# Three more seven-product steps inside one layer of a two-layer LoRA kernel, and a new order for its side work

## The chip, the cores and the metric

The kernel runs on one core of a Trainium2 chip. The metric is device time in microseconds, from start to end of one execution. Three executions of the kernel before took 425.69, 426.36 and 426.70 us; the median is 426.36.

## What is computed

Two layers, each added to its input, in float32, on 8 sequences of 256 tokens with 1024 features.

```python
base   = x @ W.T                                   # W: 1024 x 1024
logits = x @ Wr.T + 5.0 * one_hot(language_ids[b]) # 8 experts
gates  = softmax over the two largest logits, zero elsewhere
h      = A[e] @ x                                  # e = 1..8, rank 16
x      = x + base + 2.0 * sum_e gates[e] * (B[e] @ h[e])
x      = x + x @ weight[adapter_ids[b]].T          # one 1024 x 1024 matrix per sequence
```

## The kernel before, in words

**Blocks.** Tokens, inner dimension and outputs are each cut in two, so the large product of layer one is a 2 x 2 by 2 x 2 block product. The blocks of x are `xb["11"]` to `xb["22"]`, those of W `wb[...]`, the results `yb[...]`. An identity is added to the diagonal blocks of W, so that adding x comes for free.

**Three levels of steps.** The block product is done with seven block products instead of eight (a Strassen-Winograd step); they are named 1, 2, 5, 6, 3, 7, 4 in the order in which they run. Product 1 is `opening` (L563), the others are `product` (L655). Each is itself such a step, with seven smaller products of 256 x 256 x 1024 blocks. Inside `product` these are P1 to P7 with sums s1 to s4 and t1 to t4, made on VectorE (DVE), and they accumulate in three PSUM pairs called A, X and B, which change their places from product to product (`roles`, L110). A small product is two k chunks by two row chunks, that is four matmuls of 512 columns. B3 and A4 are names of the small products that finish quarter 1 (in B) and quarter 2 (in A); A6 and A7 are P6 and P7, B5 is P5, X2 is P2.

**Third steps.** A few of the small products are cut once more: `third` (L412) replaces four 512-column matmuls by seven `piece`s of 256 columns (L449). It needs eight sums of its own on DVE: r1, r2, r4 (128 columns each) and q1, q2, q4 (256 columns) first, and r3, q3 once piece 5 has been read; and `take` (L467) evicts pieces 1, 6, 7 and 5 separately. "Leaf 2" is a third step on the small product with a(0,1) and b(1,0), "leaf 3" the one that is B3 (the small product P3), "leaf 4" the one that is A4. Pieces 1, 6 and 7 share a PSUM bank (`single0`, or one half of X), so piece 6 waits until piece 1 has been evicted, and piece 7 until piece 6 has. Before, twelve small products are cut so: leaves 3 and 4 in product 1, leaf 2 in products 2, 6 and 7, leaves 2, 3 and 4 in product 5, leaves 2 and 4 in products 3 and 4 (L994 to L1038).

**The order of the work.** Every engine runs its queue in order, and the order is fixed when the program is built. PE's order is the order of the calls in `product`. DVE's is made by a small planner (L346 to L393): `now["pe"]` and `now["dve"]` are estimated clocks, `queue` holds sums with a cost and the events that they need, `ahead(until)` fills DVE's time up to PE's clock with whatever is free, `force(key)` pulls a sum in when PE needs it, and `after` puts an eviction behind PE's clock. Costs and events only decide the order; at run time semaphores keep engines apart.

**Gates.** `project` (L248) computes h and the logits on PE for tokens (j, c), `take(j, c)` (L265) adds the language bias on DVE and copies h on ScalarE (ACT), `gating(j)` (L290) is 20 small operations that end with the scaling of h, and `turn(j)` (L323) transposes h with eight matmuls on PE and copies it to `hg`, where the LoRA matmuls (L551, `hg,b_sb` and `hg,bdiff`) read it. The first gates are turned before product 2, the second after it, in two single banks, `ps_g`.

**Other sums.** I22 adds an identity to w22, S1 forms w21 - w22, S2, S3 and S4 form other blocks of W, `bdiff` holds differences of the LoRA matrix. Before, I22, S1 and bdiff are queued with product 2's work (L1012 to L1014).

**Layer two** (`adapt`, L851) does one sequence after the other with one such step each. Its weights are loaded by SyncE (SP) into blocks of x and w that layer one has finished with (`load_w1`, L804), its sums for the first sequence are `prep_w1` and `prep_y0`. GpSimd (POOL) issues the DMAs that add: `add_x`, `add_raw` and `join`.

The calls in the order of time, with what is queued ahead of each:

```python
queue += [(0.69, (), "I22", lambda: add_identity(wb["22"]))]
queue += w_sum(minus, "21", "22", "21", (), "S1")
queue += [(2.0, (), "bdiff", b_differences)]
queue += make_subs("5", "21", "12", (2, 3, 4), ("T1",), "2", 1)
product("2", y21, y11, 0, 0)
force(gates)
turn(1, singles("ps_g_1"))
```

Of the kernel before, what the change touches and what calls it, by code (L numbers as in the profile page):

```python
# [25 lines left out]
def kernel(  # L26
# [43 lines left out]
    TQ = TH // 2  # L70
# [32 lines left out]
    def singles(name):  # L103
        return [single(f"{name}{v}", v) for v in range(2)]
# [185 lines left out]
    def gating(j):  # L290

        m1, hot1, ops1 = first_max(lg[j], j, 1)
        rest = rtile([P, C, E], "rest")
        m2, hot2, ops2 = first_max(rest, j, 2)
        dm = rtile([P, C], "dm")
        ex = rtile([P, C], "ex")
        den = rtile([P, C], "den")
        g1 = rtile([P, C], "g1")
        g2 = rtile([P, C], "g2")
        wide = [P, C, E]  # L300

        def onto_h():
            h = hT[j].rearrange("p c (e r) -> p (c e) r", r=R)
            g = hot1.rearrange("p c e -> p (c e)").unsqueeze(2).to_broadcast([P, C * E, R])
            tt(h, h, g, ALU.mult)


        ops = ops1 + [
            lambda: nc.vector.scalar_tensor_tensor(rest, hot1, NEG, lg[j], ALU.mult, ALU.add)
        ] + ops2 + [  # L310
            lambda: minus(dm, m2, m1),
            lambda: nc.scalar.activation(ex, dm, AF.Exp),
            lambda: nc.vector.tensor_scalar(den, ex, 1.0, None, ALU.add),
            lambda: nc.vector.reciprocal(g1, den),
            lambda: nc.vector.tensor_scalar(g1, g1, SCALING, None, ALU.mult),
            lambda: tt(g2, g1, ex, ALU.mult),
            lambda: tt(hot1, hot1, g1.unsqueeze(2).to_broadcast(wide), ALU.mult),
            lambda: tt(hot2, hot2, g2.unsqueeze(2).to_broadcast(wide), ALU.mult),
            lambda: add(hot1, hot1, hot2),
        ]  # L320
        return [(0.23, f) for f in ops] + [(1.22, onto_h)]

    def turn(j, banks):  # L323

# [21 lines left out]
    events = {}  # L346
    queue = []
    done = {}

    def us(n):  # L350
        return (n + 151) / 960

    def vec(t, fn, key=None):
        fn()
        now["dve"] += t
        done[key] = now["dve"]

    def event(name, later=0.0):
        events[name] = now["pe"] + later
# [5 lines left out]
    def ahead(until):  # L365

        while now["dve"] < until:
            may = [(t, i) for i, t in enumerate(map(free, queue)) if t is not None and t < until]
# [43 lines left out]
    def third(key, leaf, lhs, rhs, place, what):  # L412
# [10 lines left out]
        def op(name, tag, fn, x, y, what):  # L423
            width = P if name[0] == "r" else NQ

            def run():
                if place == 0:
                    t[name] = sub3.tile([P, width], F32, name=f"{name}_{key}{leaf}", tag=tag)
                else:
                    t[name] = spare(1536 + (place - 1) * 1152 + at[tag], width)  # L430
                fn(t[name], *(t[v] if isinstance(v, str) else v() for v in (x, y)))

            return us(width), what, f"{me}.{name}", run
# [42 lines left out]

        return ops, ops3, piece, take

    def make_subs(key, w, x, leaves=(), what=(), last=(), place=0):

# [5 lines left out]
        def a(i, j):  # L486
            return wb[w][:, 2 * j : 2 * j + 2, i * OQ : (i + 1) * OQ]
# [27 lines left out]
        if 3 in leaves:  # L515
            deep[3] = third(key, 3, lambda: t["s2"], lambda: b(1, 1), 1, (f"{key}:P6",))
        if 4 in leaves:
            deep[4] = third(key, 4, lambda: a(1, 1), lambda: t["t2"], 2, (f"{key}:P6",))
        subs[key] = (a, b, t, late, deep)
        return [  # L520
            op("s1", add, a(1, 0), a(1, 1), what),
# [17 lines left out]
    def multiply(up=None, tokens=None):  # L539


        def mm(acc, lhs, rhs, first=False, rows=None, c=0, part=(0, 1), ms=(0, 1), need=()):
            if rows == "d":
                force("bdiff")
            for key in need:
                force(key)
            steps = [(lhs[:, k, ts(m, P)], rhs[:, k, :], m) for k in part for m in ms] if part else []
            if up is not None and rows is not None:
                steps += [(up[rows][:, ts(m, P)], hg[tokens][:, c, :], m) for m in ms]
            for i, (l, r, m) in enumerate(steps):  # L550
                nc.tensor.matmul(  # L551
                    acc[:, m, :],
                    lhsT=l,
                    rhs=r,
                    start=(first and i < len(ms)),
                    stop=(i >= len(steps) - len(ms)),
                    skip_group_check=True,
                )
                now["pe"] += 0.859

        return mm

    def opening(key, dest):  # L563
# [56 lines left out]
        chunk(1)  # L620
        piece(6)
        out(6, q1, q1)
        chunk(2)
        for n in (2, 3, 4):
            piece(n, B)
# [1 line left out]
        piece(7)  # L627
        out(7, q1, q1)
        last_out = out
        ops, ops3, piece, out = third(key, 4, lambda: a(1, 1), lambda: t["t2"], 0, ())  # L630
        for o in ops[:2]:
            vec(o[0], o[3], o[2])
        last_out(5, q1, q1)
        for o in ops[2:]:
            vec(o[0], o[3], o[2])
        add(q1, B, q1)
        chunk(4)
        piece(1)
        out(1, q2)
        chunk(5)  # L640
        piece(5)
        for o in ops3:
            vec(o[0], o[3], o[2])
# [5 lines left out]
        chunk(7)  # L649
        piece(7)  # L650
        out(7, q2)
        out(5, q2, q2)
        add(q2, A, q2)

    def product(key, base, dest, lora=None, tokens=None, sub=False, joined=None):  # L655

# [61 lines left out]
        if 4 in deep:  # L718
            _, _, piece4, take4 = deep[4]
            piece4(1)  # L720
            take4(1, at[2], old[2], sub)
        if 3 in deep:
            _, _, piece, take = deep[3]
            force(f"{key}.X2")
            piece(1, banks=halves(X))
            take(1, at[1], at[1], sub)
            force(f"{key}.B5")
            mm(B, None, None, False, "d", 1, part=())
            piece(5, banks=halves(X))
            if 4 in deep:  # L730
                piece4(5)
            piece(6)
            take(6, at[1], at[1], sub)
            if 4 in deep:
                piece4(6)
                take4(6, at[2], old[2], sub)
            for n in (2, 3, 4):
                piece(n, B)
            if 4 in deep:
                force(f"{key}.A7")  # L740
                mm(A, None, None, False, "1", 0, part=())
            piece(7)
            take(7, at[1], at[1], sub)
            take(5, at[1], at[1], sub)
        else:
            mm(B, t["s2"], b(1, 1), False, "d", 1, need=K("s4", "B5"))
        put(1, B, True, "B3")
        join(1)
        if 4 in deep:
            if 3 not in deep:  # L750
                piece4(5)
                piece4(6)
                take4(6, at[2], old[2], sub)
# [8 lines left out]
        else:  # L762
            mm(A, a(1, 1), t["t2"], False, "1", 0, need=K("t4", "A7"))
            put(2, A, name="A4")
        join(2)
        ahead(now["pe"])


# [216 lines left out]

    opening("1", y21)
    done.clear()
    now["pe"], now["dve"] = 0.0, 3.5
    after(0.4, lambda: take(0, 1))
    for i, (t, f) in enumerate(gating(0)):  # L990
        vec(t, f, "gates0")
    project(1, 0, halves(pair("ps_h_1_0", 2)))
    now["pe"] += 7.5
    subs2 = make_subs("2", "12", "21", (2,))  # L994
    run(subs2[:2])
    after(0.4, lambda: take(1, 0))
    run(subs2[2:])
# [11 lines left out]
    event("T2", 30.0)  # L1009
    queue += [(t, (), f"gate{i}", f) for i, (t, f) in enumerate(gating(1))]  # L1010
    gates = queue[-1][2]
    queue += [(0.69, (), "I22", lambda: add_identity(wb["22"]))]  # L1012
    queue += w_sum(minus, "21", "22", "21", (), "S1")
    queue += [(2.0, (), "bdiff", b_differences)]  # L1014
    queue += make_subs("5", "21", "12", (2, 3, 4), ("T1",), "2", 1)
    product("2", y21, y11, 0, 0)
    force(gates)
    turn(1, singles("ps_g_1"))
    now["pe"] += 2.0
    raw("21", 0, 1)  # L1020
    add_raw("21", 1, 1)
    event("T3", 30.0)
    queue += w_sum(add, "11", "21", "11", (), "S2")
    queue += make_subs("6", "11", "22", (2,), ("T2",), "5", 0)
    product("5", None, y22, 1, 1)
    raw("12", 1, 1)
    event("x22", 14.0)
    queue += w_sum(minus, "12", "11", "12", (), "S4")
    queue += make_subs("3", "12", "12", (2, 4), ("x22",), "6", 1)
    product("6", y21, y21, sub=True)  # L1030
    add_raw("22", 1, 0)
# [3 lines left out]
    product("3", y22, y12, 2, 1, joined=(y12, y21))  # L1035
    load_w1(0, "21", "12", "22", "11")
    event("w0", 18.0)
    queue += make_subs("4", "22", "22", (2, 4), ("T4",), "7", 1)  # L1038
    product("7", y21, y21, joined=(y22, y21))
    queue += [(t, ("w0",), f"w0_{i}", f) for i, (t, _, f) in enumerate(prep_w1(0, 0))]  # L1040
    y0 = []

    def prep_y0(i):
        y0[:] = y0 or prep_y(0)
        y0[i][2]()

    queue += [(0.69, ("4:P7", "7:join2"), f"y0_{i}", lambda i=i: prep_y0(i)) for i in range(4)]
    product("4", y21, y21, 1, 0)
    for q in list(queue):
        q[3]()  # L1050
    load_w1(1, "22", "12", "11", "21")

    for u in range(NB):
        if u + 1 < NB:
            todo += prep_y(u + 1)
            todo += prep_w1(u + 1, 4)
        adapt(u)
# [50 lines left out]
```

## Time and profile before

| | before |
|---|---|
| three executions | 425.69, 426.36, 426.70 us |
| the profiled execution | 425.69 us, of which 423.7 us are the span of the instructions |
| PE matmuls | 418.8 us busy, 1294 records |
| PE weight loads | 226.1 us busy |
| DVE | 287.6 us busy, 439 instructions |
| ACT | 40.6 us busy |
| start of product 2, 5, 6 | 59.25, 90.62, 120.28 us |
| start of product 3, 7, 4 | 143.97, 174.05, 197.67 us |
| start of layer two | 227.75 us |
| end of the last matmul | 420.3 us |

A float32 matmul shows as two records. In the timeline of PE a row is "start, length, engine, line, operation, output<-inputs, sizes, number of records"; the length of a row reaches a little past the start of the next because matmuls are pipelined, so durations are taken from start to start. In a table of windows each engine has "busy (x instructions)", in the order PE, weight loads, DVE, ACT, POOL, and the last three columns are PE's granted clock, the busy share of the DMA engines and GB/s. DVE's most frequent forms, start to start where the next follows at once: 1.13 us for 1024 columns, 0.60 for 512 (0.72 where the next reads what it wrote), 0.34 for 256, 0.20 for 128.

### The profile page before, as it was taken

What the parts mean: (1) busy time and instruction counts of PE and PEld (TensorE: products, weight loads), DVE (VectorE), ACT (ScalarE), POOL (GpSimd) and SP (SyncE); (2) the same over time, 40 slices, a digit from 0 to 9 for tenths busy, and PEclk for the clock granted to TensorE, in tenths of its full rate; (3) what the DMA queues carried; (4) which work ended last, traced back from release to release, by engine and by line L of the source; (5) the groups of instructions that cost most, each with busy time, mean ns of one, the idle gap of its engine ahead of it and who ended that gap; (6) DMA issues with size and microseconds to landing.
All of it is one profiled execution on the core that took longest, in us unless ns stands there. A gap on an engine that the chain in (4) does not pass through costs nothing.

```text
span 423.7 us, 3569 instructions
## 1 busy us (share of the span) xinstructions
PE 418.8 (99%) x1294; PEld 226.1 (53%) x1294; DVE 287.6 (68%) x439; ACT 40.6 (10%) x69; POOL 17.6 (4%) x26
## 2 busy tenths in 40 slices
PE   8999999999999999999999999999999999999996
PEld 6579975445655454554555444444444444444574
DVE  1645699957888989878786666765747666665531
ACT  2010120022110000000000101010101101010110
POOL 1000020110001101103000000000000000000000
PEclk9999999999999999999999999999999999999999
DMA  8995089476220964918902384666658385650202
GB/s 274 385 397 236 2 173 210 126 184 101 100 99 4 179 215 78 294 24 155 342 0 99 116 321 159 242 214 213 224 194 300 109 298 190 213 183 0 101 0 99
DMA packets 20257, 72.61 MB, mean 171 GB/s; under 512 B 1552, under 2 KB 3856, under 8 KB 15248
## 3 DMA queue, kind: packets, MB, share of 16 engines
q1 hardware_dynamic: 15088, 58.87, 38.0%
q0 software_dynamic: 3904, 12.58, 16.6%
q10 hardware_dynamic: 1248, 0.93, 0.7%
q8 instruction: 10, 0.16, 0.1%
q14 instruction: 7, 0.06, 0.0%
HBM read 55.61 MB, written 8.39 MB: 151 GB/s over the span
## 4 chain that ended last, share of the span: by engine, by line
PE 99%; POOL 0%; ACT 0%; issue 0%; POOLq 0%
PE A L863 23%; PE A L551 21%; PE B L551 13%; PE B L863 13%; PE ps_h L256 7%; PE X L863 6%; PE P L463 5%; PE A_last L930 3%; PE X L551 3%; PE X L463 2%; PE A L463 1%; PE idle L568 1%; PE B L463 1%; PE ps_g L326 0%; ACT z L960 0%
## 5 line engine op out<-in xcount | busy, mean ns | idle before, releaser
L551 PE MATMUL A<-t,s 128*128 128x512 f32 x112 | 50.3, 592 | 0.0
L863 PE MATMUL B<-x,x 128*128 128x512 f32 x96 | 43.2, 592 | 0.0
L863 PE MATMUL A<-w,x 128*128 128x512 f32 x88 | 39.6, 592 | 0.0
L228 DVE TENSOR_TENSOR w<-w,w 128x1024 f32<-128x1024 f32 x24 | 29.1, 1223 | 15.1 <-PE A L863 15.1
L863 PE MATMUL A<-w,y 128*128 128x512 f32 x88 | 39.1, 592 | 0.0
L256 PEld LDWEIGHTS ps_h<-y,x 128*128 128x128 f32 x256 | 31.7, 190 | 3.3 <-issue 2.9
L551 PEld LDWEIGHTS A<-t,s 128*128 128x128 f32 x112 | 21.2, 190 | 21.2 <-issue 20.6
L256 PE MATMUL ps_h<-y,x 128*128 128x136 f32 x256 | 31.9, 279 | 0.0
L863 PEld LDWEIGHTS B<-x,x 128*128 128x128 f32 x96 | 18.2, 190 | 22.1 <-issue 22.0
L863 PEld LDWEIGHTS A<-w,x 128*128 128x128 f32 x88 | 16.7, 190 | 21.0 <-issue 21.0
L863 PEld LDWEIGHTS A<-w,y 128*128 128x128 f32 x88 | 16.7, 190 | 20.6 <-issue 20.6
L228 DVE TENSOR_TENSOR y<-P,y 128x512 f32<-128x512 f32 (+1 forms) x31 | 17.6, 567 | 14.0 <-PE P L463 9.1
L228 DVE TENSOR_TENSOR y<-A,y 128x1024 f32<-128x1024 f32 x17 | 20.8, 1223 | 8.3 <-issue 4.6
L551 PE MATMUL A<-x,w 128*128 128x512 f32 x56 | 25.4, 594 | 0.0
L551 PE MATMUL B<-x,s 128*128 128x512 f32 x40 | 18.0, 592 | 0.0
L228 DVE TENSOR_TENSOR x<-w,x 128x1024 f32<-128x1024 f32 (+1 forms) x11 | 10.6, 968 | 10.8 <-PE A L863 7.8
L225 ACT ACTIVATE z<-A 128x512 f32<-128x512 f32 x12 | 7.2, 597 | 101.4 <-PE A L863 101.4
L228 DVE TENSOR_TENSOR w<-x,w 128x1024 f32<-128x1024 f32 x8 | 9.7, 1225 | 10.2 <-PE A L863 5.7
L551 PEld LDWEIGHTS A<-x,w 128*128 128x128 f32 x56 | 10.3, 190 | 10.8 <-issue 10.5
L228 DVE TENSOR_TENSOR z<-z,X 128x512 f32<-128x512 f32 x7 | 4.8, 687 | 15.9 <-PE X L863 15.9
L551 PE MATMUL B<-t,s 128*128 128x512 f32 x32 | 15.0, 595 | 0.0
L863 PE MATMUL X<-w,y 128*128 128x512 f32 x32 | 14.4, 592 | 0.0
(179 smaller groups left out, 555.8 us busy)
## 6 DMA issues: line engine op xcount, KB each, us to landing
x<-w_dram SPq DMA_DIRECT2D x24, 1024.0 KB, 5.1
x<-xT_dram SPq DMA_DIRECT2D x10, 1024.0 KB, 10.6
w<-w_dram SPq DMA_DIRECT2D x8, 1024.0 KB, 4.8
out_dram<-z SPq DMA_DIRECT2D x15, 512.0 KB, 3.0
x<-x POOLq DMA_DIRECT2D x4, 1024.0 KB, 9.9
x<-xT_dram POOLq DMA_DIRECT2D x4, 1024.0 KB, 9.3
y<-y POOLq DMA_DIRECT2D x8, 512.0 KB, 5.3
w<-wT_dram SPq DMA_DIRECT2D x3, 1024.0 KB, 15.3
```

The lines of the kernel that those rows point to most:

```text
L225: nc.scalar.activation(out_, x, AF.Copy, scale=scale)
L228: nc.vector.tensor_tensor(out_, x, y, op)
L256: nc.tensor.matmul(ps[v][:, u * EA : (u + 1) * EA], lhsT=xk(k, j, c)[:, ts(r, P)], rhs=aw_sb[:, k, :], start=(first and k == some[0] and u ...
L463: nc.tensor.matmul(out_, lhsT=l, rhs=r, start=(n in (1, 5)), stop=True, skip_group_check=True)
L551: nc.tensor.matmul(acc[:, m, :], lhsT=l, rhs=r, start=(first and i < len(ms)), stop=(i >= len(steps) - len(ms)), skip_group_check=True,)
L568: nc.tensor.matmul(idle[:, 0, :P], lhsT=ident, rhs=ident, start=True, stop=True)
L863: nc.tensor.matmul(accs[name], lhsT=lhs[:, k // 2, k % 2, :], rhs=rhs[:, k, :], start=(first and k == 0), stop=(k == KH - 1), skip_group_c ...
L930: nc.tensor.matmul(acc, lhsT=lhs[:, k // 2, k % 2, :], rhs=rhs[:, k, ts(v, m)], start=(first and k == 0), stop=(k == KH - 1), skip_group_c ...
```

## The change

- **Third steps.** Product 2 and product 6 get leaf 4, product 4 gets leaf 3. Product 2's small sums lie in a part of `yb["12"]` (place 3).
- **The opening.** The six first sums of its leaf 4 are made before piece 2 of leaf 3, in `yb["12"]`; piece 1 of leaf 4 comes one projection chunk later; I22, S1 and bdiff are made at the end of the opening, ahead of the last two evictions.
- **The second gates** are turned within product 2, between A7 and B3, in the two halves of X's pair.
- **A held queue.** From the start of a product's leaf 3 to its end only sums whose key begins with that product's number may run ahead (`hold`). Layer two's first sums are renamed so that they count as product 4's.
- **Order inside `product`.** Piece 7 of leaf 3 and its evictions come before A's LoRA rows, and B3 is issued in two halves with leaf 4's pieces 5 and 6 behind them where there is no leaf 3.
- **The queue.** S4 stands ahead of product 5 instead of product 3. The planner's costs are changed (n + 66 instead of n + 151 cycles, and others).
- **Layer two** starts with X and B exchanged in the rotation of the PSUM pairs.

```diff
-        return [(0.23, f) for f in ops] + [(1.22, onto_h)]
+        return [(0.26, f) for f in ops] + [(us(2 * TQ), onto_h)]
...
+    hold = [""]
     def us(n):
-        return (n + 151) / 960
+        return (n + 66) / 960
...
             may = [
                 (t, i)
                 for i, t in enumerate(map(free, queue))
+                if t is not None and t < until and queue[i][2][0] in (hold[0] or queue[i][2][0])
             ]
...
+                elif place == 3:
+                    t[name] = flat(yb["12"])[:, 2048 + at[tag] : 2048 + at[tag] + width]
...
         out(6, q1, q1)
+        next_leaf = third(key, 4, lambda: a(1, 1), lambda: t["t2"], 3, ())
+        for o in next_leaf[0]:
+            vec(o[0], o[3], o[2])
         chunk(2)
...
         chunk(4)
+        chunk(5)
         piece(1)
         out(1, q2)
-        chunk(5)
         piece(5)
...
         out(7, q2)
+        add_identity(wb["22"])
+        for f in w_sum(minus, "21", "22", "21"):
+            f[3]()
+        b_differences()
         out(5, q2, q2)
         add(q2, A, q2)
...
+        if between is not None:
+            between(X)
         if 3 in deep:
+            hold[0] = key
...
             for n in (2, 3, 4):
                 piece(n, B)
+            piece(7)
+            take(7, at[1], at[1], sub)
+            take(5, at[1], at[1], sub)
             if 4 in deep:
                 force(f"{key}.A7")
                 mm(A, None, None, False, "1", 0, part=())
-            piece(7)
-            take(7, at[1], at[1], sub)
-            take(5, at[1], at[1], sub)
+        elif 4 in deep:
+            mm(B, t["s2"], b(1, 1), False, "d", 1, ms=(0,), need=K("s4", "B5"))
+            piece4(5)
+            mm(B, t["s2"], b(1, 1), False, "d", 1, ms=(1,))
+            piece4(6)
+            take4(6, at[2], old[2], sub)
         else:
             mm(B, t["s2"], b(1, 1), False, "d", 1, need=K("s4", "B5"))
...
+        hold[0] = ""
         ahead(now["pe"])
...
-    subs2 = make_subs("2", "12", "21", (2,))
+    subs2 = make_subs("2", "12", "21", (2, 4), early=True)
...
-    queue += [(0.69, (), "I22", lambda: add_identity(wb["22"]))]
-    queue += w_sum(minus, "21", "22", "21", (), "S1")
-    queue += [(2.0, (), "bdiff", b_differences)]
...
-    product("2", y21, y11, 0, 0)
-    force(gates)
-    turn(1, singles("ps_g_1"))
-    now["pe"] += 2.0
+
+    def turn_1(X):
+        force(gates)
+        turn(1, halves(X))
+        now["pe"] += 1.8
+
+    product("2", y21, y11, 0, 0, between=turn_1)
...
     queue += w_sum(add, "11", "21", "11", (), "S2")
-    queue += make_subs("6", "11", "22", (2,), ("T2",), "5", 0)
+    queue += make_subs("6", "11", "22", (2, 4), ("T2",), "5", 0)
+    queue += w_sum(minus, "12", "11", "12", (), "S4")
     product("5", None, y22, 1, 1)
...
-    queue += w_sum(minus, "12", "11", "12", (), "S4")
...
-    queue += make_subs("4", "22", "22", (2, 4), ("T4",), "7", 1)
+    queue += make_subs("4", "22", "22", (2, 3, 4), ("T4",), "7", 1)
...
+    role[1:] = role[2], role[1]
     for u in range(NB):
```

More of the change, by code (lines that the diff above doesn't have):

```diff
@@ L355, in vec @@
         now["dve"] += t
-        done[key] = now["dve"]
+        done[key] = now["dve"] + 0.1
     def event(name, later=0.0):
@@ L367, in ahead @@
         while now["dve"] < until:
-            may = [(t, i) for i, t in enumerate(map(free, queue)) if t is not None and t < until]
+            may = [
+                (t, i)
+                for i, t in enumerate(map(free, queue))
+                if t is not None and t < until and queue[i][2][0] in (hold[0] or queue[i][2][0])
+            ]
             ready = [i for t, i in may if t <= now["dve"]]
@@ L477, in third, with make_subs @@
         return ops, ops3, piece, take
-    def make_subs(key, w, x, leaves=(), what=(), last=(), place=0):
+    def make_subs(key, w, x, leaves=(), what=(), last=(), place=0, early=False):
         before = (f"{last}:P7",) if last else ()
@@ L517, in make_subs @@
         if 4 in leaves:
-            deep[4] = third(key, 4, lambda: a(1, 1), lambda: t["t2"], 2, (f"{key}:P6",))
+            deep[4] = third(key, 4, lambda: a(1, 1), lambda: t["t2"], 3 if early else 2, (f"{key}:P6",))
         subs[key] = (a, b, t, late, deep)
@@ L542, in mm @@
         def mm(acc, lhs, rhs, first=False, rows=None, c=0, part=(0, 1), ms=(0, 1), need=()):
-            if rows == "d":
-                force("bdiff")
             for key in need:
@@ L629, in opening @@
         last_out = out
-        ops, ops3, piece, out = third(key, 4, lambda: a(1, 1), lambda: t["t2"], 0, ())
-        for o in ops[:2]:
-            vec(o[0], o[3], o[2])
+        ops, ops3, piece, out = next_leaf
         last_out(5, q1, q1)
-        for o in ops[2:]:
-            vec(o[0], o[3], o[2])
         add(q1, B, q1)
         chunk(4)
+        chunk(5)
         piece(1)
         out(1, q2)
-        chunk(5)
         piece(5)
@@ L651, in opening, with product @@
         out(7, q2)
+        add_identity(wb["22"])
+        for f in w_sum(minus, "21", "22", "21"):
+            f[3]()
+        b_differences()
         out(5, q2, q2)
         add(q2, A, q2)
-    def product(key, base, dest, lora=None, tokens=None, sub=False, joined=None):
+    def product(key, base, dest, lora=None, tokens=None, sub=False, joined=None, between=None):
         a, b, t, late, deep = subs.pop(key)
@@ L750, in product @@
             if 3 not in deep:
-                piece4(5)
-                piece4(6)
-                take4(6, at[2], old[2], sub)
                 force(f"{key}.A7")
@@ L987 @@
     done.clear()
-    now["pe"], now["dve"] = 0.0, 3.5
+    now["pe"], now["dve"] = 0.0, 6.0
     after(0.4, lambda: take(0, 1))
@@ L1037 @@
     event("w0", 18.0)
-    queue += make_subs("4", "22", "22", (2, 4), ("T4",), "7", 1)
+    queue += make_subs("4", "22", "22", (2, 3, 4), ("T4",), "7", 1)
     product("7", y21, y21, joined=(y22, y21))
-    queue += [(t, ("w0",), f"w0_{i}", f) for i, (t, _, f) in enumerate(prep_w1(0, 0))]
+    queue += [(t, ("w0",), f"4.w{i}", f) for i, (t, _, f) in enumerate(prep_w1(0, 0))]
     y0 = []
@@ L1045, in prep_y0 @@
         y0[i][2]()
-    queue += [(0.69, ("4:P7", "7:join2"), f"y0_{i}", lambda i=i: prep_y0(i)) for i in range(4)]
+    queue += [(0.6, ("4:P7", "7:join2"), f"4.y{i}", lambda i=i: prep_y0(i)) for i in range(4)]
     product("4", y21, y21, 1, 0)
```

## The prediction

> **What bounds the kernel now.** I read the page first: busy shares, the clock row, the chain that ended last.
>
> ```profile
> span 423.7 us, 3569 instructions
> PE 418.8 (99%) x1294; PEld 226.1 (53%) x1294; DVE 287.6 (68%) x439; ACT 40.6 (10%) x69; POOL 17.6 (4%) x26
> ...
> PEclk9999999999999999999999999999999999999999
> ...
> PE 99%; POOL 0%; ACT 0%; issue 0%; POOLq 0%
> ```
>
> PE is the bound from end to end at full clock, and the chain is PE's own queue. What is left, 4.9 us, is 1.4 before the first matmul and 3.4 after the last, so inside there is next to nothing to win but matmul time; and every microsecond that PE comes to wait is lost in full. So I need two things: what the matmuls cost, and whether DVE, whose queue is in order, still delivers in time. PE's timeline gives the first, and the few places where PE is late today:
>
> ```profile
> 37.65 0.70 PE L463 MATMUL P<-t,w 128*128 128x256 f32 x2
> ...
> 84.59 3.60 PE L551 MATMUL A<-t,w 128*128 128x512 f32 x8
> 88.03 1.88 PE L551 MATMUL A<-hg,b_sb 128*128 128x512 f32 x4
> 89.74 1.04 PE L326 MATMUL ps_g<-ident,y 128*128 128x128 f32 x8
> ...
> 113.39 0.59 PE L463 MATMUL X<-x 128*128 128x256 f32 x2
> ...
> 116.41 1.88 PE L551 MATMUL A<-hg,b_sb 128*128 128x512 f32 x4
> ...
> 120.28 3.66 PE L551 MATMUL A<-x,w 128*128 128x512 f32 x8
> ```
>
> Ends overlap the next start, so I take starts. A whole small product (four 512-column matmuls, two records each) is 88.03 - 84.59 = 3.44 us. A third step is seven 256-column pieces: 116.41 - 113.39 = 3.02 us. The lone P<-t,w took 0.56 in the chain where its like take 0.43, and the eight records from 120.28 to 123.78 took 3.50 against 3.43.
>
> **Third steps, 12 to 15.** Product 2's and 6's A4 and product 4's B3 each turn from four 512-column matmuls into seven 256-column ones (counted in the two instruction lists: 388 to 376 and 116 to 137). Gain 3 x (3.44 - 3.02) = 1.25 us, all of it on PE. LoRA rows and transposes keep their number.
>
> A rule speaks against this. The Trainium skill (TensorE: Matmul & The Clock Gate, Back-to-back issue gap) says that in a stream of weight loads and matmuls the spacing is set by both operations. A third step has 14 loads where the whole product has 8, and a load record is 190 ns here. Were loads not hidden, a step would be 14 x 190 + 3020 = 5.7 us against 8 x 190 + 3440 = 5.0, and the three would lose 2.2 us. The row decides: seven pieces end to end, with their loads, at 0.43 each, so loads hide in 215 ns slots with 25 ns to spare.
>
> **PE waits that go.** The P<-t,w wait (0.13) ended with DVE's P7 eviction at 37.59; now two LoRA chunks stand before that piece. Product 6's start (0.07) waited for the X eviction ending at 120.17; P3's last piece now comes before A's LoRA rows, so that eviction ends near 118.0 against a start at 119.7. Together 0.20. Next late there is nothing on PE.
>
> **DVE work.** Each new step adds 4 sums of 128 columns and 4 of 256, a P1, a P6, a P7 and a P5 eviction. Starts of neighbours give 0.20, 0.34 and 0.72 us: 2.2 + 0.7 + 1.4 = 4.3, in all 13 us on DVE's 288. That is free only as long as nothing that PE wants stands behind it, so I walked DVE's queue in the new order, each instruction at the later of its predecessor's end and PE's end + 0.20 us (the lag in today's rows: A done at 69.56, its eviction begun at 69.76).
>
> *Opening.* I22, S1 and bdiff (0.72 + 2 x 1.13 + 1.61 = 4.6 us) move ahead of the last two evictions.
>
> ```profile
> 41.05 0.42 DVE L228 TENSOR_TENSOR q<-t 128x256 f32<-128x256 f32 x1
> 44.37 0.69 DVE L228 TENSOR_TENSOR y<-P,y 128x512 f32<-128x512 f32 x1 [2.90 <-ACT y L223]
> ```
>
> Those 2.90 us were idle; leaf 4's six sums moved into an earlier 3.15 us gap (33.7 to 36.9), so the block begins at 40.1, and the P5 eviction comes at 44.7 instead of 44.37. All behind it on DVE (first gates, product 2's sums, the takes) slips 0.36 us. PE first meets it at product 2's P1, which needs the copy of the last take: 61.25, wanted at 62.6. Slack 1.3, cost 0. The block needs w22, w21 and b_sb:
>
> ```profile
> 37.00:39.00 2.00, 2.00 (x17) 1.89 (x17) 2.00 (x6) 0.37 (x1) 0.00 (x0) 1.00 0.36 147
> 39.00:41.00 2.00, 2.00 (x16) 1.90 (x15) 2.00 (x5) 0.00 (x0) 0.00 (x0) 1.00 0.00 0
> ```
>
> The last two columns (DMA share, GB/s) fall to nothing: all loads are in before 39.0, the identity wants w22 at 40.1.
>
> *Product 2 (PE from 59.1).* The second gates no longer end in two fresh banks after the product but in X's pair before B3. The eight transposes cost 0.88 (89.74 to 90.62) in either place; ACT's two copies (0.59 each) now lie beside B3. The wait added: transposes after the X eviction. DVE has P7, P5 and X in a row from 76.1, done 78.8; PE arrives at 79.8. Gates end at 69.3, although their chain is held 1.7 us behind P1's eviction. Queued behind the transposes on PE is all of B3 and A4, so a miss would cost in full; slack 1.0. Then P6 of the new step is evicted by 87.9 (wanted 89.7), and A4 by 93.1 for product 5's B, which takes its pair at 93.9.
>
> *Product 5.* P3's P6 eviction ends 114.8, wanted 115.9. The sums of product 6 that used to fill the small products are held back: DVE then idles about 1.1 us before r3, and six sums (1.6 us) go behind A4, still before 123.9; the first, q1, is wanted at 125.3.
>
> *Product 6, the tightest.* From B's eviction at 131.5 DVE has no pause: 1.13 t4, the P7 pair with B's own 2.58, X 1.13, two sums 0.54, A7 1.13, P1 0.34, four sums 1.08, product 3's s1 0.60, r3 and q3 0.54, t1 1.13, P6 0.34. That is 10.5 us, so P6 is out at 142.1 and P7 may start; PE wants it at 142.5. Slack 0.35. Here the same page (Step-by-step, LDWEIGHTS) says PE pulls weight loads ahead of running matmuls; by that a wait that is met in time costs 0. But in the row at 37.65 the load began with its matmul, only after the wait, and 0.13 went. I take 0, being in time by more than a load of 0.19, and keep 0 to 0.5 for an error of my walk. It cannot be below 0, as no wait stands there now.
>
> *Products 3 and 7* keep their rows. S4 stands earlier in the queue but still runs in product 6 (today at 125.3 and 127.1, in the walk at 126.0 and 127.6), ahead of A's eviction at 129.4, before which DVE idled 1.74 us. *Product 4:* X is evicted at 216.2 for P3's P1 at 217.2; P3's P6 at 221.6 for P7 at 222.4; X's last eviction at 225.2 for layer two's A at 226.2. Layer two's swap gives its B the pair freed by B3 (226.3) instead of A4's (229.1), wanted at 229.7. All fit: cost 0, upper bound 0.5 together.
>
> *Other queues.* x21's second half is read 3.4 us longer (B3 ends at 86.2), so its reload on SP and the add behind it on POOL go 3.4 us later, landing near 107; the first reader is product 7's t1 past 160. Weight loads for layer two on SP wait for product 4's P3 to let go of x22 (222.4 against 221.7), used near 240. No compute instruction is new on POOL or ACT.
>
> **The sum.** 423.7 - 1.25 - 0.20 = 422.25 us of span. The profiled execution took 425.69, 1.99 more than its span; so 424.24 for it. It was the fastest of the three before; against their median of 426.36 the same 1.45 us gives 424.9, 0.34% faster. A measurement of this kernel can tell about 0.2%, here 0.85 us, from no change.
>
> **Rivals.**
> - *New just-in-time waits eat half.* At product 6's P7, P3 of product 4 or product 5's B (slacks 0.35 to 1.0) DVE comes late. For: the walk is a sum of some 20 terms between resets, and a product with 0.35 is easily short. Against: DVE meets PE's own waits again in each product, so lateness does not add up beyond one. Price 0.3 to 1.2, middle 0.7: 425.6.
> - *Slower: the opening's block stalls DVE.* If w21 lands late, S1 stands still at the head of DVE's queue with the P5 eviction, gates and takes behind it, and PE stops at product 2's P1. Each microsecond past 41 + 1.3 is a microsecond of PE. To end slower by 0.85 it must eat 1.45 + 0.85 as well: landing after 44.5. At 45.5 the kernel takes 428.2. Against it: the DMA share of zero from 39.0 on.
> - *The steps gain less than columns say* (loads show in the 25 ns margin): at half the gain 425.5. Against it: seven pieces in a row at 0.43 today.
>
> **How the numbers follow.** Forecast 0.76 (424.3 to 425.5 with the runs' own spread of half a microsecond); just-in-time waits 0.14; weaker steps 0.05; slower 0.05. Range 424.1 to 425.9. Faster by over 0.2% (under 425.5): nearly all of the first, a third of the second and third: 0.79. Same 0.16; slower 0.05.
>
> **What would show it.** Right: PE busy about 417.4 with the same 4.9 us outside; 376 matmuls of 512 columns; product 2 starts near 59.1, 5 near 90.1, 6 near 119.7, 3 near 142.9, 4 near 196.6, layer two near 226.2 (today 227.75); no wait of PE listed within the products; DVE about 300 busy. Wrong: a gap before product 6's last piece, before the transposes near 79.8, or at product 2's P1; DVE standing at S1 on a DMA near 41; pieces further apart than 0.43.

## The result and the profile after

| | before | after |
|---|---|---|
| median of 17 runs each, us | 426.11 | 424.76 |
| lowest to highest, us | 425.08 to 426.74 | 423.86 to 425.38 |
| ratio after/before, 95% interval | | 0.9971 (0.9964 to 0.9977) |
| span of the profiled execution, us | 423.7 | 422.5 |
| start of product 2 to start of layer two, us | 168.50 | 167.19 |

Faster by 0.29%. The head of the page of the changed kernel, and its chain by engine:

```profile
span 422.5 us, 3642 instructions
...
PE 417.6 (99%) x1312; PEld 229.5 (54%) x1312; DVE 299.5 (71%) x475; ACT 40.6 (10%) x69; POOL 17.6 (4%) x26
...
PEclk9999999999999999999999999999999999999999
...
PE 99%; POOL 0%; ACT 0%; issue 0%; POOLq 0%
```

PE has 1.2 us less of busy time in 18 more records, DVE has 11.9 us more in 36 more, and PE is still the bound from end to end. The only wait that the list of waits shows for PE is the one ahead of the first matmul, as before:

```profile
PE idle L573 <- POOL ident masks.py:199: 1.4, 1, 1.4
```

PE's timeline at the places that the prediction named, one row per run of like records, with start and length in us:

```profile
38.77 0.59 PE L470 MATMUL P<-t,w 128*128 128x256 f32 x2
...
59.35 1.02 PE L556 MATMUL A<-x,w 128*128 128x512 f32 x2
...
79.97 1.04 PE L326 MATMUL X<-ident,y 128*128 128x128 f32 x8
...
119.97 3.60 PE L556 MATMUL A<-x,w 128*128 128x512 f32 x8
...
142.75 0.59 PE L470 MATMUL P<-x 128*128 128x256 f32 x2
...
226.54 3.60 PE L878 MATMUL A<-w,y 128*128 128x512 f32 x8
```

The lone P<-t,w lasts 0.59 like its kind; it lasted 0.70 before. Product 6 starts with rows of 3.60 where it had 3.66. (The row at 59.35 has two records of eight because the view ends there.) From product 2 (59.35) to layer two (226.54) the work takes 167.19 us, 1.31 less than before.

That stretch is the quantity to compare, because the start of the kernel differs from execution to execution. The first rows of PE on data, in the changed kernel and in the experiment below with sums back in product 2:

```profile
4.26 2.72 PE L556 MATMUL X<-x,w 128*128 128x512 f32 x4
```

```profile
4.26 3.62 PE L558 MATMUL X<-x,w 128*128 128x512 f32 x4
```

Both start at 4.26 us, but the next row (the first projection, ps_h) starts at 6.82 in the one and at 7.72 in the other. Over the thirteen traces of this case, one per kernel, these four records take 1.82 to 3.46 us, and product 2 begins between 58.66 and 60.25 us. Their weight loads lie 0.43 us apart at the quick end and 0.85 at the slow end; 0.85 is also the distance at a granted clock of 0.50 in the kernel with the steps in the old order (from 96.11 to 98.67). That suggests a clock that is still low at the start, but the clock column says 1.00 there in all thirteen traces, so it is not shown.

From the first projection to product 2 it is 52.65 us in the two kernels with the old opening and 52.53 in the eleven with the new one. Layer two, from its first matmul to the last row of A_last, took 188.89 us before and after, and 188.89 or 188.90 in every experiment but one (the steps in the old order, 189.37). So the stretches are good to some hundredths, the total only to half a microsecond.

### The profile page after: what moved, and what is told of

Its sections match the earlier page's. It is cut to its first block, busy times and chain, and to the rows that moved or that the text cites. A ratio compares the mean times of both kernels' runs of the same rounds, so it can differ in the third digit from the quotient of the medians.

```text
span 422.5 us, 3642 instructions
## 1 busy us (share of the span) xinstructions
PE 417.6 (99%) x1312; PEld 229.5 (54%) x1312; DVE 299.5 (71%) x475; ACT 40.6 (10%) x69; POOL 17.6 (4%) x26
## 4 chain that ended last, share of the span: by engine, by line
PE 99%; POOL 0%; ACT 0%; issue 0%; POOLq 0%
PE A L878 23%; PE A L556 20%; PE B L878 13%; PE B L556 12%; PE ps_h L256 7%; PE X L878 7%; PE P L470 5%; PE A_last L945 3%; PE X L470 3%; PE X L556 3%; PE A L470 2%; PE B L470 1%; PE idle L573 1%; PE X L326 0%; PE ps_g L326 0%; ACT z L975 0%
## 5 line engine op out<-in xcount | busy, mean ns | idle before, releaser
L228 DVE TENSOR_TENSOR y<-P,y 128x512 f32<-128x512 f32 (+1 forms) x35 | 19.8, 566 | 7.5 <-PE P L470 5.7
L556 PE MATMUL B<-x,s 128*128 128x512 f32 x32 | 14.9, 592 | 0.0
L228 DVE TENSOR_TENSOR x<-x 128x1024 f32<-128x1024 f32 (+1 forms) x15 | 14.7, 1005 | 0.0
```

Source lines behind the costliest of these rows:

```text
L228: nc.vector.tensor_tensor(out_, x, y, op)
L556: nc.tensor.matmul(acc[:, m, :], lhsT=l, rhs=r, start=(first and i < len(ms)), stop=(i >= len(steps) - len(ms)), skip_group_check=True,)
```

## The experiments

**Theory:** the three third steps give 1.25 us, two PE waits 0.2, and all of DVE's extra work stays out of PE's way; the new order earns little and is there so that the steps find DVE free. **Rivals:** the order brings the gain; or just-in-time waits eat part of it; or a wait that is met shortly before PE arrives costs something all the same.

| kernel | median, us | ratio to before (95%) | product 2 to layer two, us | less the changed kernel's |
|---|---|---|---|---|
| before | 426.11 | | 168.50 | +1.31 |
| changed | 424.76 | 0.9971 (0.9964 to 0.9977) | 167.19 | 0 |
| new order, 12 steps | 425.89 | 0.9995 (0.9987 to 1.0003) | 168.43 | +1.24 |
| old order, 15 steps | 431.47 | 1.0128 (1.0113 to 1.0144) | 174.17 | +6.98 |
| gates after product 2 | 425.45 | 0.9993 (0.9985 to 1.0002) | 168.48 | +1.29 |
| sums back in product 2 | 426.36 | 1.0010 (1.0002 to 1.0018) | 169.01 | +1.82 |
| no hold | 424.71 | 0.9975 (0.9964 to 0.9985) | 167.19 | 0.00 |
| pairs not swapped | 424.63 | 0.9968 (0.9958 to 0.9978) | 167.20 | +0.01 |
| sixteen steps | 424.38 | 0.9966 (0.9952 to 0.9981) | 166.88 | -0.31 |
| one idle sum more | 425.00 | 0.9976 (0.9967 to 0.9985) | 167.31 | +0.12 |
| three idle sums more | 425.77 | 0.9990 (0.9983 to 0.9997) | 168.23 | +1.04 |
| twelve idle sums more | 432.90 | 1.0158 (1.0143 to 1.0174) | 174.32 | +7.13 |
| twelve, placed earlier | 432.75 | 1.0148 (1.0130 to 1.0165) | 174.83 | +7.64 |

Each ratio is taken against runs of the kernel before from the same occasion, so it is not the quotient of two medians of this table. Each stretch comes from one trace.

### The order without the steps

```
-    subs2 = make_subs("2", "12", "21", (2, 4), early=True)
+    subs2 = make_subs("2", "12", "21", (2,))
...
-    queue += make_subs("6", "11", "22", (2, 4), ("T2",), "5", 0)
+    queue += make_subs("6", "11", "22", (2,), ("T2",), "5", 0)
...
-    queue += make_subs("4", "22", "22", (2, 3, 4), ("T4",), "7", 1)
+    queue += make_subs("4", "22", "22", (2, 4), ("T4",), "7", 1)
```

> The changed kernel with the three new third steps taken back (twelve, as before), and all of the new order kept. Theory: the gain is the matmul time of the steps, 3 x 0.42 = 1.25 us, and only 0.20 comes from PE waits that the order removes. So 1.2 to 1.3 us slower than the changed kernel, about 426.0, that is 0.2 under the kernel before; layer two starts near 227.8. Rival: it is the new order that gains, by emptier queues; then it stays within 0.3 us of the changed kernel, 424.8 to 425.1.

Measured: 425.89 us, no different from before (0.9995), and the stretch is 168.43 us. Against the changed kernel that is 1.24 us for three steps, 0.41 each; against before it is 0.07, the one wait of product 6 that lies in this stretch, and the opening ahead of it has the other 0.12 (52.53 against 52.65). By itself the order earns the two waits and no more.

### The steps without the order

The kernel before, with the three lists of leaves of the changed one and the buffer that product 2's leaf 4 needs:

```
+                elif place == 3:
+                    t[name] = flat(yb["12"])[:, 2048 + at[tag] : 2048 + at[tag] + width]
...
+    subs2 = make_subs("2", "12", "21", (2, 4), early=True)
...
+    queue += make_subs("6", "11", "22", (2, 4), ("T2",), "5", 0)
...
+    queue += make_subs("4", "22", "22", (2, 3, 4), ("T4",), "7", 1)
```

> The kernel before with the three new third steps alone; sums, gates, hold and the order inside product as before. Theory: the steps are worth 1.25 us of PE, but DVE cannot cover them in product 2: bdiff is ready 0.6 us after B3 wants it, piece 7 of the new step waits about 1.0 for its eviction and sums, and the transposes of the second gates, in the two banks of the small pieces, wait about 3 us for their two evictions. Together 3.5 to 5 us slower than before, near 430. Rival: the steps gain by themselves and the new order only tidies; then 424.9 to 425.2.

Measured: 431.47 us, 5.4 over before, where 3.5 to 5 was expected. Against the changed kernel, product 2 is 4.44 us longer, product 5 1.70, products 6 and 3 together 0.84. PE's timeline at the end of product 2, with the idle time before a row and its releaser in brackets:

```profile
89.30 0.59 PE L465 MATMUL A<-y,w 128*128 128x256 f32 x2
91.25 0.70 PE L465 MATMUL P<-y 128*128 128x256 f32 x2 [1.36 <-DVE y L228]
94.13 1.38 PE L326 MATMUL ps_g<-ident,y 128*128 128x128 f32 x8 [2.18 <-DVE y L228]
95.35 4.87 PE L553 MATMUL A<-x,w 128*128 128x512 f32 x7
```

DVE's queue says why. While these pieces run it is still taking the sums of the product that follows (r, q, s, t), with the evictions and the last sums that PE waits for behind them. The first gap ends with the sum at 90.78, the second with the evictions at 93.39:

```profile
90.25 0.42 DVE L228 TENSOR_TENSOR y<-P,y 128x256 f32<-128x256 f32 x1
...
90.78 0.42 DVE L228 TENSOR_TENSOR y<-t 128x256 f32<-128x256 f32 x1
...
92.25 1.22 DVE L228 TENSOR_TENSOR t<-x 128x1024 f32<-128x1024 f32 x1
93.39 1.41 DVE L228 TENSOR_TENSOR y<-P,y 128x512 f32<-128x512 f32 x2
```

The last row of PE is worth a second look: seven records take 4.87 us where eight take 3.60. The granted clock was at 0.50 from 95.4 to 98.9 us, and that is the 1.70 of product 5, which the expectation did not count; it is taken up below. Which part of the order keeps the 0.84 away is not shown.

### The gates' transposes after product 2

```
-        turn(1, halves(X))
+        turn(1, singles("ps_g_1"))
...
-    product("2", y21, y11, 0, 0, between=turn_1)
+    product("2", y21, y11, 0, 0)
+    turn_1(None)
```

> The changed kernel with the second gates turned after product 2, in the two banks that the small pieces use. Theory: the transposes wait for the evictions of pieces 7 and 5 (PE done, 0.2 us, then 0.72 each), so product 5 starts 1.2 to 1.4 us later than in the changed kernel, and the whole takes about 426.0. Rival: the place of the transposes does not matter, as their time on PE is the same; then 424.8.

Measured: the stretch is 1.29 us longer; the total, with its spread, shows 0.7 of that by the medians and 0.9 by the ratios. PE's row in this kernel:

```profile
89.85 1.38 PE L326 MATMUL ps_g<-ident,y 128*128 128x128 f32 x8 [0.78 <-DVE y L228]
```

At the end of the product two fresh banks come free only with DVE's last P evictions (89.11 to 90.53): the transposes wait 0.78 us, then the second half waits again (1.38 against 1.04). In X's pair, in the middle of the product, the same eight transposes run without a wait. The move is worth as much as all three steps, but only once product 2 ends in small pieces: in the kernel before, the transposes at 89.74 waited for nothing.

### The sums for the lower half back in product 2

```
-        add_identity(wb["22"])
-        for f in w_sum(minus, "21", "22", "21"):
-            f[3]()
-        b_differences()
...
+    queue += [(0.69, (), "I22", lambda: add_identity(wb["22"]))]
+    queue += w_sum(minus, "21", "22", "21", (), "S1")
+    queue += [(2.0, (), "bdiff", b_differences)]
```

> The changed kernel with I22, S1 and bdiff queued with product 2 as before, not at the end of the opening. Theory: in DVE's order bdiff ends near 84.5 us, B3's first LoRA row wants it at 82.6; PE waits 1.9 us there and the kernel takes about 426.7. Rival: DVE has room in product 2 or later products take the delay up; then within 0.3 us of the changed kernel.

Measured: the stretch is 1.82 us longer, 1.35 in product 2 and 0.47 in product 5. Theory had 1.9 at the one place in product 2; that the total comes out so close is luck, as the rest was lost at a place that it did not name. PE's rows in this kernel:

```profile
84.70 1.13 PE L558 MATMUL B<-hg,bdiff 128*128 128x512 f32 x2 [1.07 <-DVE bdiff L228]
...
96.79 1.98 PE L558 MATMUL B<-x 128*128 128x512 f32 x4 [0.21 <-DVE y L228]
```

These 4.6 us of DVE don't fit into product 2 beside a second set of third-step sums. In the opening they cost nothing.

### No hold; pairs not swapped

```
-            hold[0] = key
+            hold[0] = ""
```

> The changed kernel with the hold taken out: VectorE's planner may again take any product's sums while P3's small products run; everything else stays. Theory (VectorE has room wherever a sum isn't wanted within a few tenths of a us, so the hold by itself is worth nothing): within 0.2 us of the changed kernel, 424.6 to 425.0, and no new wait of TensorE; product 6's B keeps about 0.5 us. Rival (the hold is what lets the third steps of product 5 and 6 run without a wait): a wait of 0.3 to 1.0 us on VectorE ahead of a small product of P3 or ahead of product 6's B, 425.1 to 425.8.

```
-    role[1:] = role[2], role[1]
```

> The changed kernel with layer two's PSUM pairs not swapped: its B takes the pair that product 4's last result (A4) leaves last. That result is out of PSUM at about 229.4 us, and B is wanted at 229.97. Theory: the swap hides nothing that was in the way; within 0.2 us of the changed kernel, 424.6 to 425.0, and layer two's B starts without a wait. Rival (the eviction of 1.22 us slips as the opening's did, by 0.5 us and more): B waits 0.1 to 0.5 us, 424.9 to 425.3, and after.product 4's last result would show as the releaser.

Measured, each by itself: 167.19 and 167.20 us, the changed kernel's 167.19, and no wait. In the kernel without the swap, A's last eviction still clears B's pair in time (PE reaches B at 230.76, half a microsecond behind the end of this DVE row):

```profile
228.98 1.22 DVE L228 TENSOR_TENSOR y<-A,y 128x1024 f32<-128x1024 f32 x1
```

So of the four parts of the order that were taken back alone, two pay for the steps (the opening's block and the turned gates) and two do nothing that a trace can show. The others (the order inside `product`, leaf 4's sums earlier in the opening, S4's place and the planner's costs) were not taken back alone, so what each of them is worth is not known.

### A sixteenth step

```
-    queue += make_subs("7", "21", "21", (2,), ("T3",), "3", 0)
+    queue += make_subs("7", "21", "21", (2, 4), ("T3",), "3", 0)
```

> A sixteenth third step: leaf 4 of product 7 too. Theory (each step takes one 512-column pass of 0.42 us off TensorE as long as VectorE's extra work, about 4.3 us, lies beside it): 0.42 us less than the changed kernel, 424.35, TensorE without a new wait; the narrowest places are product 4's B pair (0.4 us) and the last small product of product 4's P3 (0.2 us). Rival (VectorE has no room left ahead of product 4): a wait of 0.3 to 1.0 us in product 4 takes the gain, 424.7 to 425.4.

Measured: 424.38 us, the lowest median of all. Its interval overlaps the changed kernel's; the traces separate the two: product 7 is 0.42 us shorter (23.21 against 23.63), product 4 is 0.10 longer; the whole stretch is 0.31 shorter. The 0.10 lies in two rows of this kernel's PE timeline, 0.65 and 0.63 long where pieces of their kind take 0.59, though neither is listed as a wait:

```profile
219.29 0.65 PE L470 MATMUL X<-x 128*128 128x256 f32 x2
...
222.38 0.63 PE L470 MATMUL X<-x 128*128 128x256 f32 x2
```

The timeline of weight loads shows what they are; such loads normally come in pairs of 0.41 us that begin 0.22 us ahead of their matmul:

```profile
219.25 0.30 PEld L470 LDWEIGHTS X<-x 128*128 128x128 f32 x2 [0.62 <-DVE y L228]
...
222.31 0.30 PEld L470 LDWEIGHTS X<-x 128*128 128x128 f32 x2 [0.17 <-DVE x L228]
```

The load began only when DVE was done, 0.04 to 0.07 us ahead of its matmul instead of 0.22, and the first of the piece's two records has to wait for it.

### One idle sum ahead of the tightest place

```
             piece4(6)
+            if key == "6":
+                for _ in range(1):
+                    add(spare(3840, 256), wb["11"][:, 0, :256], wb["11"][:, 1, :256])
             take4(6, at[2], old[2], sub)
```

> The changed kernel with one useless sum of 256 columns (0.34 us of VectorE) put ahead of the evictions in product 6; its result is not used. The narrowest place of the walk is there: the eviction that frees the buffer of the last small product ends at 142.37 us and TensorE gets there at 142.75, so the margin falls from 0.38 to 0.04 us. Theory (a wait that ends before TensorE gets there costs nothing): 0 to 0.05 us, 424.7 to 424.9. Rival (a weight load can't be pulled ahead past a wait that is still open, as at 37.65 us of the kernel before, where 0.13 us was lost): the load, which began 0.22 us ahead of its matmul, begins late and 0.13 to 0.2 us is lost, a gap ahead of the matmul at 142.75; 424.9 to 425.1.

Measured: 0.12 us lost. The matmul itself is on time to 0.02 us, 0.45 behind its neighbour, and yet the next product starts 0.53 behind it instead of 0.43. PE's timeline of this kernel, and then its weight loads:

```profile
142.93 0.59 PE L470 MATMUL A<-x,w 128*128 128x256 f32 x2
143.38 0.70 PE L470 MATMUL P<-x 128*128 128x256 f32 x2
143.91 3.60 PE L556 MATMUL A<-x,w 128*128 128x512 f32 x8
```

```profile
142.71 0.41 PEld L470 LDWEIGHTS A<-x,w 128*128 128x128 f32 x2
143.37 0.30 PEld L470 LDWEIGHTS P<-x 128*128 128x128 f32 x2 [0.26 <-DVE y L228]
```

The rival is right and the theory fell: a wait that ends 0.04 us ahead of PE's arrival is not free. It costs about 0.1 us: the load began 0.05 us after the wait's end and 0.01 ahead of its matmul, where 0.22 is usual.

### Three and twelve idle sums

The same sums three and twelve times, this time right ahead of the eviction itself; then twelve at the place of the single one (the diff above with 12).

```
+            if key == "6":
+                for _ in range(3):
+                    after(0, lambda: add(spare(3840, 256), wb["11"][:, 0, :256], wb["11"][:, 1, :256]))
             take4(6, at[2], old[2], sub)
```

> The changed kernel with three useless sums of 256 columns (0.335 us each) on VectorE right ahead of the eviction that frees the buffer of product 6's last small product (it ended at 142.37 us, TensorE got there at 142.75); their result is not used. Theory (past the margin of 0.38 us every tenth of VectorE is a tenth of TensorE, and a load that is late adds 0.1): the eviction ends at 143.38, a gap of 0.6 to 0.65 us, 0.75 us lost, 425.5. Rival (the delay is passed on: the eviction of B and those behind it come late for product 3 as well): a second gap behind it, 1.0 us and more lost, 425.8 or more.

> The same with twelve sums (4.0 us): one long gap of TensorE of about 3.65 us ahead of product 6's last small product, which is as much as the two gaps (1.36 and 2.18 us) behind which the clock fell to 0.50 in the kernel with the steps in the old order. Theory 1 (the clock goes by the idle share of the last few us): it falls here too, some us behind the gap, and 1.5 to 1.9 us are lost beside the gap: 430.0 to 430.4. Theory 2 (it takes an idle time broken by work, or something else of that kernel): the clock stays at 1.00 and 3.8 us are lost: 428.5.

> The same twelve sums, put ahead of the operands of product 6's third and fourth small product: two gaps, about 1.6 us ahead of the third and 2.0 us ahead of the last, with 0.9 us of work between them; in sum as idle as one gap of 3.6 us. Theory 1 (the clock goes by the idle share of the last few us, however it is split): the clock falls as with the one long gap, 430.0 to 430.4. Theory 2 (only a long unbroken gap counts): 1.00 here, 428.5 to 428.7, whatever the one long gap does.

Measured for three: 1.04 us lost, all of it at this place, and none behind it. These sums, which all write the same buffer, follow each other every 0.46 us, not every 0.335 as expected (in the kernel with twelve, the row of twelve takes 5.48 us). The row of three begins at 142.07 and the eviction behind it at 143.32, so three cost DVE 1.25; less the margin of 0.38 that is 0.87, and the late load adds 0.17. The theory holds with these two prices. Twelve cost DVE 5.40.

The kernel with twelve loses 7.13 us in its trace: the piece starts 5.09 us late (147.14 against 142.05), and the other 2.04 are lost while PE works. Placed earlier the sums make two gaps, 2.83 and 1.81 us, 4.98 us late in sum, and 2.66 are lost while PE works. PE's timeline of the kernel with twelve:

```profile
147.14 1.22 PE L470 MATMUL P<-x 128*128 128x256 f32 x2 [4.92 <-DVE y L228]
148.15 5.06 PE L556 MATMUL A<-x,w 128*128 128x512 f32 x8
```

The busy time by stretches of a tenth has the granted clock in the third column from the right. In the same kernel it falls during the gap and comes back 4 us after work did:

```profile
144.20:144.30 0.10, 0.00 (x0) 0.00 (x0) 0.10 (x1) 0.00 (x0) 0.00 (x0) 0.83 0.67 102
144.30:144.40 0.10, 0.00 (x0) 0.00 (x0) 0.10 (x1) 0.00 (x0) 0.00 (x0) 0.50 0.59 102
151.00:151.10 0.10, 0.10 (x1) 0.05 (x1) 0.10 (x2) 0.00 (x0) 0.00 (x0) 0.53 0.00 0
151.10:151.20 0.10, 0.10 (x1) 0.00 (x0) 0.10 (x1) 0.00 (x0) 0.00 (x0) 1.00 0.00 0
```

The clock fell in both kernels with twelve sums, behind a gap of 2.83 us too, so theory 2 is out. Theory 1 is not shown in full: in the last 3.4 us ahead of each fall the idle time was one piece (the last section), so whether two shorter pieces count together is open. The times are over its 430.0 to 430.4: the four runs of each lie from 431.04 to 433.25 and from 431.66 to 433.11 us. The price of the sums accounts for 1.4 of that; the rest, up to 1.5 in the median, stays open. The profiled execution of the first was its fastest run, with the quickest start of all traces (1.82 us for the first four records), and only that one was traced.

## Why the prediction was right

It gave 424.9 us; 424.76 was measured. The median before came out at 426.11 with all runs, not 426.36, so the better test is the difference: 1.45 forecast, 1.35 between the medians, and 1.31 + 0.12 = 1.43 between the two traces from the first projection to layer two. By its steps:

- **Third steps, 1.25 us.** 1.24 by the order-only kernel. Read at its worst, with no load hidden, the page that speaks against it (spacing set by loads and matmuls) would have meant a loss of 2.2 us; the new pieces run at 0.43 each with their loads, so the row was the one to follow.
- **PE waits, 0.20 us.** Both are gone: 0.07 in the stretch and 0.12 in the opening (52.53 against 52.65 from the first projection). The profiled execution hides the second: its first four records took 2.56 us where they took 2.43 before, and began 0.09 later, so product 2 starts at 59.35, not at 59.1, and all later starts are 0.2 to 0.35 behind the forecast ones.
- **Next late on PE: nothing.** Right. Turn of gates: X out at 78.98, PE there at 79.97, slack 0.99 for a forecast of 1.0. Product 6: the row of DVE below ends at 142.37 with PE at 142.75, slack 0.38 for 0.35. Layer two's B pair: free at 226.57, wanted at 229.97.

```profile
77.76 1.22 DVE L228 TENSOR_TENSOR y<-X,y 128x1024 f32<-128x1024 f32 x1
...
141.96 0.41 DVE L228 TENSOR_TENSOR y<-y,P 128x256 f32<-128x256 f32 x1
```

- **Opening, DVE's slip of 0.36 us.** Mis-sized: it was 1.02 by the trace's time and 0.92 against PE, which began product 2 0.10 later. The P5 eviction came at 44.98 (0.51 late against PE, not 0.33), and the one behind it waited another 0.52 where 0.11 was usual:

```profile
44.98 0.68 DVE L228 TENSOR_TENSOR y<-P,y 128x512 f32<-128x512 f32 x1
46.19 1.22 DVE L228 TENSOR_TENSOR y<-A,y 128x1024 f32<-128x1024 f32 x1 [0.52 <-DVE y L228]
```

The gap of 0.51 to 0.52 stands in every trace that has the block of I22, S1 and bdiff there, and not in the one kernel with the new opening but without the block (0.11); what it waits for stays open. It cost nothing: ACT's copies of the last take are out at 62.19, and product 2's P1 starts at 62.78. The forecast slack of 1.3 was 0.6.

- **A wait met in time costs 0, with 0 to 0.5 kept.** Right for this change, as the margin was 0.38 and a load begins 0.22 ahead. As a rule it is wrong nearer than that (the last section has the numbers): the prediction weighed the skill's pull-ahead of weight loads (TensorE: Matmul & The Clock Gate, Step-by-step) against one row with 0.13 lost, and the runs side with the row. With the margin at 0.04, 0.12 was lost, and with sixteen steps 0.10 in two places. The 0 to 0.5 was kept for an error of the walk, not for this.
- **The hold, the swap and the other queues at no cost.** Right for all of them together: no wait came. The hold and the swap bring nothing either; the other queues were not tried alone.
- **The rivals.** Just-in-time waits did not come with this change; they came as soon as one of the two other parts was taken back (1.3 and 1.8 us). The slower rival's place was the opening's loads, which were in before 39.0 again. What the order really guards against lies in the middle and at the end of product 2, and is more than that rival's example (1.8 over before): the steps in the old order end 5.4 over it.

## What to carry over

When one engine is the bound from end to end, a trade of its time for another engine's is priced by the other's queue, not by its share of busy time: walk that queue to each place where the bound engine takes something from it. Keep the walk's margin above some 0.2 us, since a wait that ends closer to the bound engine's arrival cost up to 0.12 here although no wait is listed. And take the order of work and the steps it makes room for as one change: apart, the order gave 0.19 us and the steps lost 5.4, together 1.4 came of it.

## What had not been expected of the hardware

**The clock falls after gaps of two microseconds, and stays down in whole windows.** Worked out from the tenths at the edges (0.74 and 0.69, 0.83 and 0.53, 0.94 and 0.92), the clock was at 0.50 from 95.448 to 98.862 in the kernel with the steps in the old order, from 144.266 to 151.094 with twelve sums, and from 146.288 to 153.116 with twelve placed earlier: 3.414, 6.828 and 6.828 us, once and twice the same length. That is the free-running window of about 3.4 us that the Trainium skill gives (TensorE: Matmul & The Clock Gate, What's actually happening). The page has the clock fall after a window that is idle; here the 3.414 us ahead of the three falls were idle for only 2.10, 2.06 and 2.34 us (PE rows: 92.03 to 94.13, 142.21 to 144.27, 142.87 to 145.21), 60 to 69%. A window idle for 1.82 us (53%) kept the low clock in the last of the three; one idle for 1.44 us (42%) ahead of the first did not bring it down. So the line lies somewhere between, as far as three traces show. In each of the three windows ahead of a fall the idle time is one piece. A window of work at half the clock costs 1.7 us: with the steps in the old order, product 5's first eight records took 5.13 us by their starts (95.35 to 100.48) instead of 3.43. Gaps listed as 0.78 us (three sums) and 1.07 us (sums back in product 2) left the clock alone and cost 1.04 and 1.35 us in all.

**A wait can cost time without being listed as one**, as in the kernels with one idle sum and with sixteen steps: it stands on the weight loads' row, not on the matmuls'. How much follows from the traces. PE is "due" where its row before ends by starts (for one idle sum 142.93 + 0.43); the loss is what the piece starts late and what it takes beyond its usual time.

| kernel, place | wait ended | PE due | margin | lost | sum |
|---|---|---|---|---|---|
| before, P<-t,w | 37.59 | 37.63 | 0.04 | 0.12 | 0.16 |
| before, product 6 | 120.17 | 120.28 | 0.11 | 0.07 | 0.18 |
| sixteen steps, first | 219.20 | 219.29 | 0.09 | 0.07 | 0.16 |
| sixteen steps, second | 222.26 | 222.37 | 0.11 | 0.04 | 0.15 |
| one idle sum | 143.32 | 143.36 | 0.04 | 0.12 | 0.16 |
| three idle sums | 143.73 | 142.85 | -0.88 | 1.04 | 0.16 |

The second row rests on the prediction's reading that product 6 waited for the X eviction; its load's row names PE. Margin and loss add up to about 0.16 us in all six, so by this estimate a wait is free only when it ends some 0.16 us before PE is due. A margin of 0.27 fits: in the changed kernel's product 4 an eviction ended at 219.37, its piece began at 219.64, and nothing was lost.
